# Two block products of the first expert product, each by seven products of their own blocks

## The chip, the cores and the metric

The kernel runs on one core of a Trainium2 chip. Its time is device microseconds (us) of one execution, the median over runs. The engines are TensorE (PE for matmuls, PEld for its weight loads), VectorE (DVE), ScalarE (ACT), GpSimd (POOL) and SyncE (SP, which issues most DMAs). Each engine works through its own queue; semaphores order the queues among each other. Matmuls write PSUM[...].

## The reference

A modulated projection of `x` gives the token rows `y` (4096 rows of 512). A router scores each row for 8 experts; every expert takes the 1024 rows that it scores highest, and adds its gated two-layer network to them:

```python
scores = jax.nn.softmax(xt @ Wr, axis=-1)
G, idx = jax.lax.top_k(scores.T, k)
X_in = xt[idx]
h = jax.nn.gelu(jnp.einsum('ekd,edh->ekh', X_in, W1) + b1[:, None, :], approximate=False)
X_e = jnp.einsum('ekh,ehd->ekd', h, W2) + b2[:, None, :]
contrib = (G[..., None] * X_e).reshape(E * k, D)
out = jnp.zeros((N, D), dtype=x.dtype).at[idx.reshape(-1)].add(contrib)
```

All of it is float32. Here k = 1024, D = 512 and the hidden width is 2048.

## The kernel before

The first 180 us or so make `y`, the scores and the rows of expert 0. After that the kernel is a row of 16 equal passes: 8 experts, and for each expert two halves `p` of the hidden width. A pass is a **hidden stage** (`X_in @ W1` for 1024 hidden columns, bias and Gelu into the buffer `H`) and an **output stage** (`H @ W2`, scaled by the gate and added to the output rows by an indirect DMA).

Both products are done as 2 x 2 blocks by seven block products in place of eight (Winograd's form). For the hidden stage the token matrix is split into two halves of 512 tokens and two of 256 inputs, the weights into two halves of inputs and two of 512 hidden columns. DVE makes four sums of token blocks once an expert (`left_sums`, called from `prepare`, line 948) and four sums of weight blocks per pass (`weight_sums`, line 195). The last one is made in place, in block `0,1`.

A hidden stage is four units (`hidden_unit`, line 342 on), each 128 of the 512 columns of a half. A unit is seven products, in the order p1, p2, p6, p7, p5, p3, p4. Each product is two matmuls of 128 x 512 (inputs 0 to 127 and 128 to 255). p1, p6, p5 and p3 add up in one bank `a`; ACT copies the bank out between them (`snap`, line 1059). p2 has bank `b`, p7 and p4 share a bank `c`. DVE adds the copies to `b` and `c`, and ACT's Gelu writes the four quarters of `H`. An output unit (`out_unit`, line 1102, four per pass) has the same form: seven products of four matmuls of 128 x 256, with sums of `H` blocks in four tiles of its own.

The helper `in_turns` (line 1012) sets the order on PE: p1 of a unit, then p3 of the unit before, p2, p4 of the unit before, p6, p7, p5. At the end of a stage the last p3 and p4 are issued. Between units it calls other work: the sums of the weights that come next, `fetch` (indices and gathers of the next expert's rows, in the hidden stage of `p` = 1) and `prepare` (in the output stage of `p` = 1). Every matmul of both stages stands in `product` (line 1028), so the profile gives them all that line, and the tiles tell them apart: `ps_a_h`, `ps_b_h`, `ps_c_h` in a hidden stage, `ps_a_o`, `ps_b_o`, `ps_c_o` in an output stage. A scheduling layer can move an instruction past others of its engine; the order in the profile is what it left.

`fetch` first makes the indices: DVE builds a one-hot tile `oh` of 32 x 128 columns (line 849), and PE multiplies it in 32 small bfloat16 matmuls. Then eight indirect DMAs gather rows into `row` tiles (four buffers), SP writes them to a DRAM tile and reads them back in a layout for DVE's transposes. The main loop loads `W1` of the next pass after the hidden stage and `W2` of the next pass after the output stage (lines 1222 and 1228).

Of the kernel before, what the change touches and what calls it, by code (L numbers as in the profile page):

```python
# [20 lines left out]
P = 128  # L21
# [4 lines left out]
def tile_modulated_expert_choice_ffn(  # L26
# [75 lines left out]
    NL = P // E  # L102
    pk = const.tile([P, P], I32, name="pk")
    nc.gpsimd.iota(pk, pattern=[[0, P]], base=0, channel_multiplier=1)
    pm = const.tile([P, P], I32, name="pm")
    nc.gpsimd.iota(pm, pattern=[[1, P]], base=0, channel_multiplier=0)
    ek = const.tile([P, P], I32, name="ek")
    nc.vector.tensor_scalar(ek, pk, E - 1, None, op0=ALU.bitwise_and)
    em = const.tile([P, P], I32, name="em")
    nc.vector.tensor_scalar(em, pm, E - 1, None, op0=ALU.bitwise_and)  # L110
    same = const.tile([P, P], BF16, name="same")
    nc.vector.tensor_tensor(same, ek, em, ALU.is_equal)
    ahead = const.tile([P, P], BF16, name="ahead")
    nc.vector.tensor_tensor(ahead, pk, pm, ALU.is_lt)
    nc.vector.tensor_mul(ahead, ahead, same)

# [47 lines left out]
    U = HP // 2  # L164
    QD = D // 2
    w1_blocks, w2_blocks = {}, {}

# [27 lines left out]
    def weight_sums(kind, blk, name):  # L195
        for _ in weight_sum_steps(kind, blk, name):
            pass

    def load_w1(e, ps):
# [537 lines left out]
    def route_others():  # L737

        ST = rt.tile([P, 2, P], F32, tag="ST", name="ST")
        ps = ps_t.tile([P, 2, P], F32, tag="t", name="ps_ST")  # L740
# [13 lines left out]

        mark = rt.tile([P, 2, P], F32, tag="run", name="mark")
        cand = two_bits[:, 0, :]
# [17 lines left out]
        def ranks(mask, name):  # L774

            run = rt.tile([P, 2, P], F32, tag="run", name=f"run_{name}")
            nc.vector.tensor_tensor_scan(run.rearrange("p h t -> p (h t)"),
# [14 lines left out]

        sel = rt.tile([P, 2, P], F32, name="sel")
        cnt = rt2.tile([P, 1], BF16, tag="cnt", name="cnt_gt")
        nc.vector.tensor_scalar(sel, ST, thr, None, op0=ALU.is_gt, op1=ALU.add, accum_out=cnt)
        tot = total(cnt, "gt")
        eq = rt.tile([P, 2, P], F32, name="eq")
        nc.vector.tensor_scalar(eq, ST, thr, None, op0=ALU.is_equal)
# [18 lines left out]
        for h in range(2):  # L817
            nc.tensor.transpose(ps[:, h, :], pos[:, h, :], ident)

        pos_i = rt.tile([P, NT, E], I32, tag="ST", name="pos_i")  # L820
        nc.vector.tensor_scalar(pos_i.rearrange("p t e -> p (t e)"),
                                ps.rearrange("p h m -> p (h m)"), -1.0, None, op0=ALU.add)
        part = rt.tile([P, NT, E], I32, tag="part", name="part")
        nc.vector.tensor_scalar(part, pos_i, P - 1, None, op0=ALU.bitwise_and)
        lo = rt.tile([P, NT, E], BF16, name="lo")
        nc.vector.tensor_copy(lo, part)
        part2 = rt.tile([P, NT, E], I32, tag="part", name="part2")
        nc.vector.tensor_scalar(part2, pos_i, 7, None, op0=ALU.logical_shift_right)
        hi = rt.tile([P, NT, E], BF16, name="hi")
        nc.vector.tensor_copy(hi, part2)  # L830
        for e in range(1, E):
            places[e] = lo[:, :, e], hi[:, :, e]

    def indices(e):
# [13 lines left out]
        )  # L848
        nc.vector.tensor_tensor(  # L849
            oh, lo.unsqueeze(2).to_broadcast([P, NT, P]),  # L850
            iota_lo.unsqueeze(1).to_broadcast([P, NT, P]), ALU.is_equal,
        )
        ps = ps_small.tile([P, 2, KG], F32, tag="small", name=f"ps_idx{e}")
# [50 lines left out]
    def gather(e, i):  # L904
# [5 lines left out]
        for j in range(GH):  # L910
            g = i * GH + j
            to = gp.tile([P, YW], F32, tag="row", name=f"row_{e}_{g}", bufs=4)
            sent = nc.gpsimd.indirect_dma_start(
                out=to[:, :], out_offset=None, in_=y_dram[:, :],
                in_offset=bass.IndirectOffsetOnAxis(ap=idx[:, e, g : g + 1], axis=0),
            )
            nc.sync.dma_start(rows[j * P : (j + 1) * P, :], to)
# [18 lines left out]
    def token_tiles(e):  # L936
# [7 lines left out]
        return xT, s, gain, ngain  # L944

    def prepare(e):

        xT, s, gain, ngain = token_tiles(e)
        for i in range(2):
            xg = gathered.pop((e, i))  # L950
            for k in range(2):
                nc.vector.transpose(
                    xT[i, k].rearrange("p j (t b) -> p t j b", b=TB),
                    xg[:, :, 2 * k * TB : 2 * (k + 1) * TB].rearrange("p t (j a) -> p t j a", a=TB))
        nc.vector.tensor_scalar_mul(ngain, gain, -1.0)
        left_sums(xT[0, 0], xT[0, 1], xT[1, 0], xT[1, 1], s)

    def first_tokens(started):
# [39 lines left out]

    def in_turns(units, between):

# [4 lines left out]
        for n in range(len(units)):  # L1005
# [12 lines left out]
            for work in between.get(n, ()):  # L1018
                with tc.issue_after(mark.ins):
                    work()  # L1020
            held = unit[5:]
        for f in held:
            f()

    def product(ps, lefts, rights, start):
        n = len(lefts)
        for k in range(n):
            nc.tensor.matmul(ps, lefts[k], rights[k], start=(start and k == 0), stop=(k == n - 1),  # L1028
                             skip_group_check=True)

    def hidden_unit(e, p, u, H, early=False):
# [8 lines left out]
        def mm(ps, left, right, start):  # L1040
            s = tokens[e][0]
            product(ps, [blk[right][:, k, u * P : (u + 1) * P] for k in range(2)],
                    [s[left][:, k, :] for k in range(2)], start)

        def begin(cols):
            s = tokens[e][0]
# [10 lines left out]
        def snap(n):  # L1057
            t = sp.tile([P, HALF], F32, tag=f"snap{n}", name=f"snap{n}_{name}")
            nc.scalar.copy(t, st["a"])  # L1059
# [7 lines left out]

        def p2():
            if not early:
                st["b"] = bank("b", name, 1)  # L1070
                mm(st["b"], "12", (1, 0), True)
            added = nc.vector.tensor_add(st["b"], st["b"], st["s1"])  # L1072
            nc.scalar.activation(out[0, 0], st["b"], AF.Gelu, bias=bias[0])
            return added
# [5 lines left out]
        def p7():  # L1080
            st["c"] = bank("c", name, 2)
            mm(st["c"], "s3", "t3", True)

        def p5():
# [9 lines left out]
        def p4():  # L1094
            mm(st["c"], "22", "t4", False)
            nc.vector.tensor_add(st["c"], st["c"], st["u2"])
            nc.scalar.activation(out[1, 0], st["c"], AF.Gelu, bias=bias[0])

        unit = [p1, p2, p6, p7, p5, p3, p4]
        return (begin, unit) if early else unit  # L1100

    def out_unit(e, p, v, H, b2_sb):
# [5 lines left out]
        a = {(i, k): H[:, :, k, i * HALF + c : i * HALF + c + P] for i in range(2) for k in range(2)}  # L1108
        s = {n: sp.tile([P, U, P], F32, tag=f"h{n}", name=f"h{n}_{name}")
             for n in ("s1", "s2", "s3", "s4")}  # L1110
        left_sums(a[0, 0], a[0, 1], a[1, 0], a[1, 1], s)
# [93 lines left out]
    for e in range(E):  # L1205
        b2_sb = fx.tile([P, D], F32, tag="b2", name=f"b2_{e}")
        nc.sync.dma_start(b2_sb, b2[e, :].partition_broadcast(P))
        for p in range(NP):
# [6 lines left out]
            if p == NP - 1 and e + 1 < E:  # L1215
                work[0] = [partial(fetch, e + 1)]
            units = [partial(hidden_unit, e, p, u, H) for u in range(U)]
            if e == p == 0:
                units[0:2] = [lambda unit=unit: unit for _, unit in early]
            in_turns(units, work)  # L1220
            if nxt[0] < E:
                load_w1(*nxt)
            work = {GH - 2: [partial(sums, "w1", w1_blocks, nxt)]}
            if p == NP - 1 and e + 1 < E:
                work[0] = [partial(prepare, e + 1)]
            in_turns([partial(out_unit, e, p, v, H, b2_sb) for v in range(GH)], work)
            if nxt[0] < E:
                load_w2(*nxt)

# [39 lines left out]
```

## Time and profile before

The time is 1750.95 us, the median of three runs (1750.62 to 1751.68).

| | |
|---|---|
| the profiled execution's own time | 1745.7 us |
| its span, first to last instruction | 1743.9 us |
| mean granted TensorE clock | 0.996 |
| distance of the first hidden products of two passes, `p` = 0 | 96.90 us |
| the same, `p` = 1 (with the index matmuls) | 98.01 us |

A group row of the profile has the line, engine, operation, tiles and shapes, then busy time and the mean length of one operation in ns, and the engine's idle time just before them with what ended it. A timeline row has the start in us, the length, and how many instructions are merged into it. The page's chain of waits goes back from the last instruction to what released each step.

### The profile page before, as it was taken

Reading aid. Unit: us, or ns where it says so; the run is one execution under the profiler, and the core shown is the slowest. Engines: PE = TensorE matmul, PEld = TensorE weight load, DVE = VectorE, ACT = ScalarE, POOL = GpSimd, SP = SyncE. Lnnn points to the kernel's source line nnn. Section 1 sums busy time; section 2 is a strip of 40 time slices with the busy share of each in tenths; the row PEclk is TensorE's granted clock in tenths of the full one; section 3 lists DMA queues with packets and bytes.
Section 4 is the critical chain, followed back from the end, with each engine's and each line's share of the span. In section 5 each row is a group of like instructions: output and inputs, shape, how many; then the busy total and the mean of one; then the engine's idle time right before and its main releaser. Section 6 shows DMA issues by size and latency. Waiting matters only on the chain.

```text
span 1743.9 us, 17415 instructions
## 1 busy us (share of the span) xinstructions
PE 1718.0 (99%) x6646; PEld 1136.2 (65%) x6646; DVE 830.8 (48%) x1467; ACT 480.2 (28%) x845; POOL 293.5 (17%) x238
## 2 busy tenths in 40 slices
PE   9998999999999999999999999999999999999997
PEld 5775475665748485766758485766758484756656
DVE  5885884524535254624535254614444254614341
ACT  3543312223131322222231313222231313222231
POOL 0112013020212013110312012110302012110202
PEclk9999999999999999999999999999999999999999
DMA  9625527441574237442574237432564137332403
GB/s 207 171 50 197 192 55 179 106 85 49 97 201 73 48 61 183 90 85 55 100 191 85 49 63 176 90 79 55 112 179 90 46 64 186 75 79 61 85 0 49
DMA packets 143252, 178.59 MB, mean 102 GB/s; under 512 B 16825, under 2 KB 92857, under 8 KB 143041
## 3 DMA queue, kind: packets, MB, share of 16 engines
q1 hardware_dynamic: 118240, 115.19, 24.4%
q0 software_dynamic: 24912, 62.27, 21.0%
q8 instruction: 52, 0.85, 0.2%
q14 instruction: 32, 0.25, 0.0%
q10 hardware_dynamic: 16, 0.02, 0.0%
HBM read 120.46 MB, written 65.37 MB: 107 GB/s over the span
## 4 chain that ended last, share of the span: by engine, by line
PE 93%; DVE 4%; ACT 1%; issue 1%; DMA 1%; POOL 0%; POOLq 0%; DVEq 0%; ACTq 0%
PE ps_a_o L1028 25%; PE ps_a_h L1028 23%; PE ps_c_o L1028 12%; PE ps_c_h L1028 12%; PE ps_b_o L1028 6%; PE ps_b_h L1028 6%; PE ps_ya L81 2%; PE ps_yc L81 1%; DVE oh L849 1%; PE ps_y L81 1%; ACT xmT L500 1%; DVE mark L760 1%; PE ps_yt L727 1%; PE ps_a_h_a L1028 0%; PE ps_yb L81 0%
## 5 line engine op out<-in xcount | busy, mean ns | idle before, releaser
L1156 POOL DMA_INDIRECT out<-o_o,idx x128 | 213.2, 1666 | 1246.7 <-DVE o_o L1153 497.0
L1028 PE MATMUL ps_a_o<-w_t,hs_o 128*128 128x256 f32 x1024 | 243.3, 380 | 1.2
L1028 PE MATMUL ps_a_h<-xs,w_t 128*128 128x512 f32 x496 | 233.4, 592 | 0.0
L1028 PEld LDWEIGHTS ps_a_o<-w_t,hs_o 128*128 128x128 f32 x1024 | 192.3, 190 | 33.7 <-issue 7.2
L1028 PEld LDWEIGHTS ps_a_h<-xs,w_t 128*128 128x128 f32 x496 | 94.1, 190 | 119.1 <-issue 118.5
L1059 ACT COPY snap_h<-ps_a_h 128x512 f32<-128x512 f32 x186 | 108.2, 582 | 230.0 <-PE ps_a_h L1028 227.0
L1123 ACT ACTIVATE snap_o<-ps_a_o,gain 128x256 f32<-128x256 f32 x128 | 60.6, 474 | 346.7 <-PE ps_a_o L1028 346.7
L1087 DVE TENSOR_TENSOR snap_h<-snap_h,ps_c_h 128x512 f32<-128x512 f32 x64 | 43.9, 687 | 217.5 <-ACT snap_h L1059 217.5
L1072 DVE TENSOR_TENSOR ps_b_h<-ps_b_h,snap_h 128x512 f32<-128x512 f32 x62 | 43.4, 699 | 202.6 <-PE ps_b_h L1028 202.6
L1028 PE MATMUL ps_c_o<-w,hs_o 128*128 128x256 f32 x512 | 124.2, 380 | 0.0
L1028 PE MATMUL ps_a_o<-w,H 128*128 128x256 f32 x512 | 124.0, 379 | 0.0
L1028 PE MATMUL ps_a_o<-w,hs_o 128*128 128x256 f32 x512 | 121.6, 380 | 0.0
L1028 PE MATMUL ps_b_o<-w,H 128*128 128x256 f32 x512 | 121.1, 379 | 0.0
L1028 PE MATMUL ps_a_h<-xT,w 128*128 128x512 f32 x248 | 120.7, 594 | 0.0
L1028 PE MATMUL ps_c_h<-xs,w 128*128 128x512 f32 x256 | 120.5, 593 | 0.0
L1028 PE MATMUL ps_c_h<-xT,w_t 128*128 128x512 f32 x256 | 120.5, 593 | 0.0
L1028 PE MATMUL ps_c_o<-w_t,H 128*128 128x256 f32 x504 | 119.1, 379 | 0.0
L1028 PE MATMUL ps_a_h<-xs,w 128*128 128x512 f32 x248 | 118.2, 599 | 0.0
L1028 PE MATMUL ps_b_h<-xT,w 128*128 128x512 f32 x248 | 116.8, 593 | 0.0
L1028 PEld LDWEIGHTS ps_a_o<-w,H 128*128 128x128 f32 x512 | 97.1, 190 | 27.0 <-issue 15.5
L1028 PEld LDWEIGHTS ps_a_o<-w,hs_o 128*128 128x128 f32 x512 | 95.9, 190 | 21.8 <-ACT snap_o L1123 9.2
L1028 PEld LDWEIGHTS ps_c_o<-w,hs_o 128*128 128x128 f32 x512 | 97.0, 190 | 13.9 <-issue 0.6
(277 smaller groups left out, 1983.8 us busy)
## 6 DMA issues: line engine op xcount, KB each, us to landing
w<-in_w SPq DMA_DIRECT2D x120, 512.0 KB, 4.1
rows<-row SPq DMA_DIRECT2D x56, 260.0 KB, 3.9
xg<-rows SPq DMA_DIRECT2D x56, 256.0 KB, 6.4
x<-in_x SPq DMA_DIRECT2D x28, 256.0 KB, 8.4
y_dram<-ytok SPq DMA_DIRECT2D x5, 1024.0 KB, 4.3
w<-in_w SPq DMA_DIRECT2D x32, 128.0 KB, 3.5
y_dram<-ytok POOLq DMA_DIRECT2D x12, 256.0 KB, 5.0
b<-in_b SPq DMA_DIRECT2D x8, 256.0 KB, 4.2
```

Source lines behind the costliest of these rows:

```text
L81: behind[engine] = make()
L500: nc.scalar.mul(t, t, styles[1][:, j, b : b + 1])
L727: nc.tensor.transpose(ps[:, o * P : (o + 1) * P], yT[:, o, t * P : (t + 1) * P], ident)
L760: nc.vector.tensor_scalar(mark, ST, cand[:, c + 1 : c + 2].bitcast(F32), None, op0=ALU.is_ge, op1=ALU.add, accum_out=cnt[:, c : c + 1])
L849: nc.vector.tensor_tensor(oh, lo.unsqueeze(2).to_broadcast([P, NT, P]), iota_lo.unsqueeze(1).to_broadcast([P, NT, P]), ALU.is_equal,)
L1028: nc.tensor.matmul(ps, lefts[k], rights[k], start=(start and k == 0), stop=(k == n - 1), skip_group_check=True)
L1059: nc.scalar.copy(t, st["a"])
L1072: added = nc.vector.tensor_add(st["b"], st["b"], st["s1"])
L1087: nc.vector.tensor_add(st["u4"], st["u4"], st["c"])
L1123: nc.scalar.mul(t, st["a"], scale)
L1156: nc.gpsimd.indirect_dma_start(out=last_rows[g] if e == E - 1 else out_rows, out_offset=bass.IndirectOffsetOnAxis(ap=idx[:, e, g : g + 1], ...
```

## The change

In 15 of the 16 hidden stages (all but the first) the products p2 and p4 of the four units are no longer made unit by unit. Together, p2 of all units is one product of a token block (512 tokens x 256 inputs) with a weight block (256 inputs x 512 columns), and so is p4. Each is now split once more into 2 x 2 blocks and made by seven products: 128 inputs, 256 tokens, and 2 x 128 hidden columns. A group (`second_level`) makes the seven products for 128 columns of each half, each in a single matmul of 128 x 256, and leaves the result in an SBUF tile `q`; four groups (`which` 2 and 4, `r` 0 and 1) serve a stage. Units take their quarter from `q`, in place of a bank.

`hidden_stage` is the new order: the other five products of the units 0, 2, 1, 3 fill 21 slots, and after each of the first 16 slots one step of a group follows (two products, or one). The last p3 and p4 of an output stage are kept back (`keep`) and issued in the slots of the next hidden stage; the loads of `W2` follow them there.

The sums of the second level are made on DVE: `second_sums` for the tokens, eight of 256 columns once an expert, and eight per pass in `weight_sums`. To make room, several tiles share buffers: the tokens' sums take the buffer of `xT10`, three sums of an output unit take the buffers of the hidden units' copies and the fourth is written over a block of `H`, the routing tiles of the first pass take the `row` buffers (three in place of four), and the tiles of the start are freed after use. The one-hot of `indices` is made in four pieces.

```diff
@@ weight_sums
+        if kind == "w1":
+            bases = {2: blk[1, 0], 4: blk["t4"]}
+            t = wpool.tile([P, 3 * len(bases), Q], F32, tag="w1_l2", name=f"w1_l2_{name}")
+            for m, (which, base) in enumerate(bases.items()):
+                b = {(k, j): base[:, k, j * Q : (j + 1) * Q] for k in range(2) for j in range(2)}
+                t1, t2, t4 = [t[:, 3 * m + n, :] for n in range(3)]
+                nc.vector.tensor_add(t1, b[0, 0], b[0, 1])
+                nc.vector.tensor_add(t2, t1, b[1, 1])
+                nc.vector.tensor_add(t4, t2, b[1, 0])
+                nc.vector.tensor_add(b[0, 1], b[0, 1], b[1, 1])
+                blk["l2", which] = {**b, "t1": t1, "t2": t2, "t3": b[0, 1], "t4": t4}
@@ indices
-        nc.vector.tensor_tensor(
-            oh, lo.unsqueeze(2).to_broadcast([P, NT, P]),
-            iota_lo.unsqueeze(1).to_broadcast([P, NT, P]), ALU.is_equal,
-        )
+        for n in range(4):
+            here = slice(n * NT // 4, (n + 1) * NT // 4)
+            nc.vector.tensor_tensor(
+                oh[:, here, :], lo[:, here].unsqueeze(2).to_broadcast([P, NT // 4, P]),
+                iota_lo.unsqueeze(1).to_broadcast([P, NT // 4, P]), ALU.is_equal,
+            )
@@ gather
-            to = gp.tile([P, YW], F32, tag="row", name=f"row_{e}_{g}", bufs=4)
+            to = gp.tile([P, YW], F32, tag="row", name=f"row_{e}_{g}", bufs=3)
@@ new functions
+    def second_sums(e):
+        s = tokens[e][0]
+        t = fx.tile([P, 4, Q], F32, tag="xT10", name=f"x2_{e}")
+        more = fx.tile([P, 2, Q], F32, tag="x2", name=f"x2_more_{e}")
+        free = [t[:, n, :] for n in range(4)] + [more[:, n, :] for n in range(2)]
+        for m, which in enumerate((2, 4)):
+            base = s["12" if which == 2 else "22"]
+            a = {(i, k): base[:, k, i * Q : (i + 1) * Q] for i in range(2) for k in range(2)}
+            s2 = {n: free[3 * m + j] for j, n in enumerate(("s2", "s3", "s4"))}
+            s2["s1"] = a[1, 0]
+            left_sums(a[0, 0], a[0, 1], a[1, 0], a[1, 1], s2)
+            s["l2", which] = {**s2, "11": a[0, 0], "12": a[0, 1], "22": a[1, 1]}
+
+    def second_level(e, p, which, r):
+        ...
+        def mm(tag, left, right, start):
+            if start:
+                st[tag] = (bank("b", f"q{name}", 1) if tag == "b" else
+                           ps_t.tile([P, HALF], F32, tag="t", name=f"ps_q{tag}_{name}"))[:, 0:Q]
+            product(st[tag], [blk[right][:, r * P : (r + 1) * P]], [s[left]], start)
+        ...
+        def p5():
+            mm("a", "s1", "t1", False)
+            st["u4"] = snap(4, -1.0)
+            nc.vector.tensor_sub(out[1, 1], st["u4"], st["c"])
+        ...
+        return [p1, p2, p6, p7, p5, p3, p4], q
+
+    def hidden_stage(e, p, H, between, held, then):
+        unit = {u: hidden_unit(e, p, u, H) for u in range(U)}
+        slots = []
+        for n, u in enumerate((0, 2, 1, 3)):
+            p1, _, p6, p7, p5, p3, _ = unit[u]
+            slots += [p1, held[0], p6] + ([held[1]] if n == 0 else []) + [p7, p5]
+            held = [p3]
+        ends = {5: 0, 10: 1, 15: 2, 20: 3}
+        steps, q = [], {}
+        for r in range(2):
+            for which in (2, 4):
+                g, q[which, r] = second_level(e, p, which, r)
+                steps += [g[0:2], g[2:4], g[4:5], g[5:7]]
+        finish = {3: (2, 0), 6: (2, 2), 7: (4, 0), 9: (4, 2), 12: (2, 1), 15: (4, 1), 16: (2, 3),
+                  19: (4, 3)}
+        mark = None
+        for n, f in enumerate(slots):
+            f()
+            if n == 3:
+                then()
+            for step in steps[n] if n < len(steps) else ():
+                mark = step() or mark
+            if n in finish:
+                which, u = finish[n]
+                unit[u][1 if which == 2 else 6](q[which, u % 2][:, u // 2, :])
+            for work in between.get(ends.get(n), ()):
+                with tc.issue_after(mark.ins):
+                    work()
+        for f in held:
+            f()
@@ hidden_unit
-        def p2():
-            if not early:
-                st["b"] = bank("b", name, 1)
-                mm(st["b"], "12", (1, 0), True)
-            added = nc.vector.tensor_add(st["b"], st["b"], st["s1"])
-            nc.scalar.activation(out[0, 0], st["b"], AF.Gelu, bias=bias[0])
+        def p2(other=None):
+            to = st["s1"] if other is not None else st["b"]
+            added = nc.vector.tensor_add(to, st["b"] if other is None else other, st["s1"])
+            nc.scalar.activation(out[0, 0], to, AF.Gelu, bias=bias[0])
             return added
...
         def p7():
             st["c"] = bank("c", name, 2)
             mm(st["c"], "s3", "t3", True)
+            if e or p:
+                nc.vector.tensor_add(st["u2"], st["u2"], st["c"])
...
+        def finish_p4(other):
+            nc.vector.tensor_add(st["u2"], st["u2"], other)
+            nc.scalar.activation(out[1, 0], st["u2"], AF.Gelu, bias=bias[0])
@@ out_unit
-        s = {n: sp.tile([P, U, P], F32, tag=f"h{n}", name=f"h{n}_{name}")
-             for n in ("s1", "s2", "s3", "s4")}
+        s = {n: sp.tile([P, HALF], F32, tag=f"snap{t}", name=f"h{n}_{name}").rearrange(
+            "p (k m) -> p k m", m=P) for n, t in (("s2", 1), ("s3", 2), ("s4", 4))}
+        s["s1"] = a[1, 0]
@@ main loop
-            units = [partial(hidden_unit, e, p, u, H) for u in range(U)]
             if e == p == 0:
+                units = [partial(hidden_unit, e, p, u, H) for u in range(U)]
                 units[0:2] = [lambda unit=unit: unit for _, unit in early]
-            in_turns(units, work)
+                in_turns(units, work)
+            else:
+                hidden_stage(e, p, H, work, held, partial(load_w2, e, p))
             if nxt[0] < E:
                 load_w1(*nxt)
...
-            in_turns([partial(out_unit, e, p, v, H, b2_sb) for v in range(GH)], work)
-            if nxt[0] < E:
-                load_w2(*nxt)
+            if e == p == 0:
+                work[0] = [partial(second_sums, 0)]
+            held = in_turns([partial(out_unit, e, p, v, H, b2_sb) for v in range(GH)], work,
+                            keep=nxt[0] < E)
```

## The prediction

> **What bounds the kernel now.** I read the page first: the span, the busy shares and the chain that ended last.
>
> ```profile
> span 1743.9 us, 17415 instructions
> PE 1718.0 (99%) x6646; PEld 1136.2 (65%) x6646; DVE 830.8 (48%) x1467; ACT 480.2 (28%) x845; POOL 293.5 (17%) x238
> PEclk9999999999999999999999999999999999999999
> PE 93%; DVE 4%; ACT 1%; issue 1%; DMA 1%; POOL 0%; POOLq 0%; DVEq 0%; ACTq 0%
> ```
>
> PE (TensorE) is busy 99% of the span at full granted clock, and 93% of the chain is its own work. Only fewer or shorter matmuls, or fewer PE waits, can move the time. Next, the groups by line, for the price of one operation of each width.
>
> ```profile
> L1028 PE MATMUL ps_b_h<-xT,w 128*128 128x512 f32 x248 | 116.8, 593 | 0.0
> L1028 PE MATMUL ps_b_o<-w,H 128*128 128x256 f32 x512 | 121.1, 379 | 0.0
> L1123 ACT ACTIVATE snap_o<-ps_a_o,gain 128x256 f32<-128x256 f32 x128 | 60.6, 474 | 346.7 <-PE ps_a_o L1028 346.7
> L1072 DVE TENSOR_TENSOR ps_b_h<-ps_b_h,snap_h 128x512 f32<-128x512 f32 x62 | 43.4, 699 | 202.6 <-PE ps_b_h L1028 202.6
> ```
>
> Every f32 matmul is two records (62 products of two matmuls give x248). The means 593 and 379 ns are latencies, which overlap; the price is the distance between starts, so I went to PE's timeline, at the seam between a hidden stage and its output stage.
>
> ```profile
> 510.58 1.88 PE L1028 MATMUL ps_c_h<-xs,w 128*128 128x512 f32 x4
> 512.30 1.88 PE L1028 MATMUL ps_a_h<-xs,w_t 128*128 128x512 f32 x4
> 514.02 1.03 PE L1028 MATMUL ps_a_o<-w,H 128*128 128x256 f32 x4
> 514.91 1.98 PE L1028 MATMUL ps_a_h<-xs,w 128*128 128x512 f32 x4
> 516.73 1.88 PE L1028 MATMUL ps_c_h<-xT,w_t 128*128 128x512 f32 x4
> 518.45 1.03 PE L1028 MATMUL ps_a_o<-w,H 128*128 128x256 f32 x4
> 519.31 1.89 PE L1028 MATMUL ps_b_o<-w,H 128*128 128x256 f32 x8
> 521.04 1.03 PE L1028 MATMUL ps_c_o<-w,hs_o 128*128 128x256 f32 x4
> 522.15 1.97 PE L1028 MATMUL ps_a_o<-w_t,hs_o 128*128 128x256 f32 x8
> ```
>
> From 510.58 to 514.02 are two 512-wide products: 1.717 us each, **0.858 us a matmul**. A 256-wide product (x8, four matmuls) takes 1.727 us elsewhere in the same timeline (529.99 to 531.72), **0.432 us a matmul**. The ratio is 0.503.
> The reader is also to see what is lost here: 521.04 to 522.15 is 1.11 us for work of 0.86, a wait of 0.25 us for DVE's second sum of the first output unit, and 0.10 us at 514.91 to 516.73.
>
> **The sum, part by part.**
>
> *Products.* In 15 of 16 hidden stages the products 2 and 4 of four units go: 2 x 4 x 1.717 = 13.74 us. In come 4 groups x 7 = 28 matmuls of 256 columns: 28 x 0.432 = 12.09 us. A stage saves 1.65 us, all on the chain; 15 stages **-24.7 us**. Ends for the new matmul: the trace has none that is a product by itself between 512-wide ones. From below, no row is cheaper than 0.432. From above, a weight load that isn't hidden: PEld's row is 190 ns, and 0.622 us each would add 80 us. I take 0.432: where the old stages change width (562.80, two records of 512, to 563.66; 567.14 to 568.00) the 512-wide start distance stays 0.86 us.
> A rule speaks against this. The Trainium skill, "TensorE: Matmul & The Clock Gate", section "Back-to-back issue gap", gives a stream of weight load and matmul pairs as about 81 ns at 128 columns and 131 ns at 512: narrowing saves little. A straight line puts 256 at 98 ns, a ratio of 0.75; the new matmul would then be 0.64 us (an estimate from that page), a stage 28 x 0.64 = 17.9 us against 13.7, the whole +63 us. The row says 0.503 for f32, where the 190 ns load fits under each record's 216 ns. The row decides.
>
> *The seam.* Product 4 with its late add and Gelu no longer ends the stage; the order of after has product 5 and product 3 of unit 3 last, and product 2 of the output unit ahead of product 6. From the end of product 5: ACT copy 0.8, DVE add to 1.5, Gelu to 2.3, then two DVE sums of 0.69 to 3.8; PE has 1.3 + 1.72 + 0.43 + 1.73 = 5.2 us of other work there. The 0.25 us wait and the 0.07 us after it go; the 0.13 us around the interleaved product 3 stay. 15 seams x 0.27 = **-4 us** (ends: 0 and -5).
>
> *The index matmuls.* The one-hot of 4.42 us on DVE (seven times) becomes four pieces, and the 32 small matmuls of PE become four lots between 512-wide matmuls. The nearest row for one lot is `tot_b` in the first stage: 0.03 us itself, and the next product takes 1.80 instead of 1.72, so 0.11; three more lots are 0.33. The first lot waits for the value tiles: from the end of the second group's product 2, DVE does an add (to 0.65), hot 0.42, one piece 1.1, and 0.28 + 0.42, about 3.0 us; PE has 2.6 us of work. That is a wait of 0.4 where the trace has 0.2. 7 x 0.5 = **+3.5 us** (ends: -1, if the pieces hide better, and +7).
>
> *ACT and DVE in the hidden stage.* New on ACT are 16 copies of 0.474 us = 7.6 on top of some 18.1 (12 copies, 16 Gelus): 26 of 46 us. On DVE 12 adds of about 0.48 and four of 0.69: 13.2 becomes 21.7 us. Neither is a bound in sum; what counts is who waits in the queue. Second-level accumulations come at least 2.1 us after the copy they overwrite, four times its length. The tight place is after the w2 sums (4.9 us on DVE, unmoved in slot). Behind them stand unit 1's two adds and the add of its product 4; ACT's Gelu waits for the last, and behind that Gelu stands the copy of unit 3's product 1, which product 6 must have. From the end of the fourth group's product 2: DVE is through at 9.2, the Gelu at 9.95, the copy at 10.55; PE wants it at 10.75. One more 0.1 us is in the later copy before product 3. I charge 0.15 us a stage, **+2 us** (ends: 0, and 0.5 a stage, 7).
>
> *Output stage.* On DVE eight 256-wide sums for the weights (each stage) and eight for the tokens (each expert) are new: 0.42 each, 3.4 + 3.4 us, beside 48 us of PE work of which DVE fills 25 to 29 now. They stand ahead of the add that frees bank `b`: for the third output unit I count that add done at 22.7 us, wanted at 25.9. Cost nothing; without that cover some 0.5 us, 7 times. The sum s1 written into H and the h sums in the snap buffers remove no wait and add none: their last readers are at least a unit back.
>
> *Moves.* SP: the w2 loads now stand behind the last output product, in front of the row copies as before, and land (4.1 us) some 25 us before their sums. With three row buffers instead of four the gathers run in three rounds; the first transposed rows stand behind a w1 load that waits for the middle of the stage. Cover: the second half's rows were and are queued behind the load of `w1_01`, free one and a half products before the end of the stage; issued 2 us and landed 6.4 us later they are 5 us early for DVE's transposes. If not, DVE holds the output sums and PE waits. The routing tiles in shared buffers and the scoped start tiles keep DVE's order; first loads wait for nothing: 0. The first hidden stage is unchanged on PE.
>
> Sum: -24.7 - 4 + 3.5 + 2 = **-23 us**. The profiled run was 1745.7 us (span 1743.9), so it would become 1722.5. The median of the runs shown is 1750.95, 5.3 above the profiled one; the same saving puts it at **1727.7 us**.
>
> **The rivals.**
> 1. *Slower: the narrow matmul shows its weight load.* Each of the 28 is one matmul with a semaphore wait; were the load held until the wait is met, 0.19 us x 28 x 15 = 80 us come in: 1808. The gain is gone from 23 us / 420 = 55 ns a matmul. For it: 514.91, where a just-met wait cost 0.1 us. Against: each output product begins with such a wait, and its eight records still keep 216 ns.
> 2. *The queues hold PE.* ACT's order has ten more places where a Gelu stands before a copy; 0.8 us more a stage is 12 us: 1740. For it: slack of 0.2 us at one place. Against: the other places have 0.5 us or more.
> 3. *The rows come late.* Three buffers and the loads in front cost more than 5 us; 2 us in 7 stages is 14 us: 1742. Against: DVE's transposes show no idle time before them now.
> 4. *It saves nothing*, since some 1.8 us a stage comes back in sum from 1 to 3: about 1751.
>
> **Chances.** The forecast 0.72, with its own range of 1720 to 1736 (the ends above). Rival 1: 0.07; rival 2: 0.11; rival 3: 0.05; rival 4: 0.05. The range for 8 in 10 is 1718 to 1740: the forecast and the near half of rival 2. About 0.2% (3.5 us) is what a measurement of this kernel can tell from no change. Faster 0.87, within 0.2% 0.04, slower 0.09.
>
> **What would show it.** In the profile after: 256-wide groups for the new tiles with 0.43 us between starts; a period of about 95 us without indices and 97 with them, where it is 96.9 and 98.0 now; a seam without the 0.25 us gap; four lots of index matmuls. Wrong would be: PEld idle behind the q tiles at each step (rival 1), PE waiting for the copies of h (rival 2), or DVE idle before the transposes (rival 3).

## The result, and the profile after

After took 1722.65 us (median of four runs, 1721.19 to 1724.97) where before took 1751.32 (four runs, 1750.62 to 1752.43): ratio 0.9837, 95% interval 0.982 to 0.9854, 28.7 us less. The forecast was 1727.7 us.

The page of after, with the span, the busy time and the clock by slices, and the chain of waits by engine and by line:

```profile
span 1721.7 us, 18925 instructions
PE 1692.2 (98%) x7006; PEld 1211.3 (70%) x7006; DVE 1004.0 (58%) x1912; ACT 553.1 (32%) x1085; POOL 310.4 (18%) x238
PEclk9999999999999999999999999999999999999999
PE 93%; DVE 3%; ACT 1%; DMA 1%; issue 1%; another core or an unknown queue 0%; POOLq 0%; POOL 0%; SPq 0%; DVEq 0%; ACTq 0%
```

PE lost 26 us of busy time although it has 360 more matmul records; DVE took on 173 us and ACT 73 us, and neither has a larger share of the chain than before. PE is still the bound.

The places named beforehand, in PE's timeline of after. First the second level among the 512-wide products (start, length, instructions merged):

```profile
576.81 1.88 PE L1063 MATMUL ps_a_h<-xs,w_t 128*128 128x512 f32 x4
578.52 0.59 PE L1063 MATMUL ps_qa<-x,w_l 128*128 128x256 f32 x2
578.95 0.59 PE L1063 MATMUL ps_qc<-x_more,w_t 128*128 128x256 f32 x2
579.39 1.02 PE L1063 MATMUL ps_a_h<-xT,w 128*128 128x512 f32 x2
```

The starts 578.52, 578.95 and 579.39 show that the new matmul costs 0.43 us, and the 512-wide product before it keeps its 1.71. Then the seam to the output stage:

```profile
612.47 1.46 PE L1063 MATMUL ps_a_o<-w,H 128*128 128x256 f32 x6
613.77 1.94 PE L1063 MATMUL ps_a_h<-xs,w 128*128 128x512 f32 x4
615.54 0.59 PE L1063 MATMUL ps_a_o<-w,H 128*128 128x256 f32 x2
615.98 1.89 PE L1063 MATMUL ps_b_o<-w,H 128*128 128x256 f32 x8
617.70 1.89 PE L1063 MATMUL ps_a_o<-w_t,hs_o 128*128 128x256 f32 x8
619.43 1.89 PE L1063 MATMUL ps_c_o<-w,hs_o 128*128 128x256 f32 x8
```

The third product (617.70) follows the second by 1.72; the gap of 0.25 us is gone, and of the 0.13 around product 3 only 0.05 is left (613.77 to 615.54 is 1.77).

The length of a pass is read as the distance of the first hidden products of two passes. The first rows of three passes before, one without indices and then one with them:

```profile
562.80 1.02 PE L1028 MATMUL ps_a_h<-xT,w 128*128 128x512 f32 x2
659.70 1.02 PE L1028 MATMUL ps_a_h<-xT,w 128*128 128x512 f32 x2
757.71 1.02 PE L1028 MATMUL ps_a_h<-xT,w 128*128 128x512 f32 x2
```

The same passes after:

```profile
564.32 1.88 PE L1063 MATMUL ps_a_h<-xT,w 128*128 128x512 f32 x4
659.14 1.88 PE L1063 MATMUL ps_a_h<-xT,w 128*128 128x512 f32 x4
755.30 1.88 PE L1063 MATMUL ps_a_h<-xT,w 128*128 128x512 f32 x4
```

A pass became 94.82 us without indices (96.90 before, so 2.08 less) and 96.15 with them (98.01; over the seven, 1.85 less). From the first whole hidden product to the end the profiles differ by 7 x 1.85 (passes with indices) + 2.36 + 6 x 2.08 (without; the first of these was 97.18 before) + 2.08 (the last, to the end of the span) - 0.14 (the first) = **29.7 us**. The two profiled executions differ by only 22 us: that of after reached its first whole hidden product at 200.13 us, that of before at 192.68, with the same PE program up to there. So the experiments had two questions: what makes up the 29.7, and whether the 7.45 us belong to the change.

### The profile page after: what moved, and what is told of

Read it like the earlier page. It is cut to its first block, busy times and chain, and to the rows that moved or that the text cites. A ratio compares the mean times of both kernels' runs of the same rounds, so it can differ in the third digit from the quotient of the medians.

```text
span 1721.7 us, 18925 instructions
## 1 busy us (share of the span) xinstructions
PE 1692.2 (98%) x7006; PEld 1211.3 (70%) x7006; DVE 1004.0 (58%) x1912; ACT 553.1 (32%) x1085; POOL 310.4 (18%) x238
## 4 chain that ended last, share of the span: by engine, by line
PE 93%; DVE 3%; ACT 1%; DMA 1%; issue 1%; another core or an unknown queue 0%; POOLq 0%; POOL 0%; SPq 0%; DVEq 0%; ACTq 0%
PE ps_a_o L1063 25%; PE ps_a_h L1063 25%; PE ps_c_o L1063 13%; PE ps_c_h L1063 6%; PE ps_b_o L1063 6%; PE ps_qa L1063 6%; PE ps_qc L1063 3%; PE ps_ya L81 2%; PE ps_b_q L1063 2%; PE ps_yc L81 1%; PE ps_y L81 1%; ACT xmT L514 1%; DVE spare L777 1%; PE ps_yt L741 1%; PE ps_a_h_a L1063 0%
## 5 line engine op out<-in xcount | busy, mean ns | idle before, releaser
L1294 POOL DMA_INDIRECT out<-o_o,idx x128 | 223.7, 1748 | 1140.2 <-DVE o_o L1291 488.4
L1063 PE MATMUL ps_a_o<-w_t,hs_o 128*128 128x256 f32 x512 | 121.2, 379 | 0.0
L1063 PE MATMUL ps_a_o<-w_t,H 128*128 128x256 f32 x512 | 121.2, 379 | 0.0
L1063 PE MATMUL ps_a_h<-xT,w 128*128 128x512 f32 x248 | 117.1, 594 | 0.0
L1063 PEld LDWEIGHTS ps_a_o<-w_t,H 128*128 128x128 f32 x512 | 97.1, 190 | 13.7 <-issue 0.5
L1063 PEld LDWEIGHTS ps_a_o<-w_t,hs_o 128*128 128x128 f32 x512 | 97.2, 190 | 13.2
L1063 PEld LDWEIGHTS ps_b_o<-w,H 128*128 128x128 f32 x512 | 97.2, 190 | 13.2
L1063 PEld LDWEIGHTS ps_c_o<-w_t,H 128*128 128x128 f32 x504 | 95.8, 190 | 13.0
```

Of the source, the lines that this page charges most:

```text
L1294: nc.gpsimd.indirect_dma_start(out=last_rows[g] if e == E - 1 else out_rows, out_offset=bass.IndirectOffsetOnAxis(ap=idx[:, e, g : g + 1], ...
```

## The experiments

Twelve runs in three turns; the kernels of a turn ran on one chip, beside runs of before.

| turn | kernel | median us | ratio to before, 95% |
|---|---|---|---|
| 1 | before (16 runs) | 1746.17 | |
| 1 | before again | 1746.7 | 1.0 (0.9991 to 1.0009) |
| 1 | seam alone | 1739.9 | 0.9968 (0.9955 to 0.998) |
| 1 | copy later | 1716.87 | 0.9831 (0.9818 to 0.9845) |
| 1 | one piece | 1714.54 | 0.9814 (0.9801 to 0.9828) |
| 2 | before (13 runs) | 1750.33 | |
| 2 | after again | 1721.31 | 0.9833 (0.982 to 0.9847) |
| 2 | 128 columns | 1727.07 | 0.9864 (0.9849 to 0.9879) |
| 2 | whole products | 1744.76 | 0.9967 (0.9958 to 0.9977) |
| 2 | later and one piece | 1720.54 | 0.9828 (0.9815 to 0.9841) |
| 3 | before (15 runs) | 1745.28 | |
| 3 | before beside | 1746.07 | 1.0002 (0.9993 to 1.0012) |
| 3 | after beside | 1716.39 | 0.9834 (0.9819 to 0.9849) |
| 3 | one piece again | 1713.13 | 0.9817 (0.9803 to 0.983) |
| 3 | copies twice | 1717.29 | 0.9837 (0.9822 to 0.9852) |

Before itself takes 1745 to 1746 us in two turns and 1750 in the other; so times are compared within a turn, and small differences by the distances of passes, which repeat to 0.05 us from the fourth on, except that in after a pass with indices is now and then 0.1 us longer.

### The seam alone

In before, the last unit of a hidden stage takes the order of after's end; all products stay.

```diff
+        def last_p7():
+            p7()
+            nc.vector.tensor_add(st["u2"], st["u2"], st["c"])
+        def last_p4():
+            b = bank("b", name + "_p4", 1)
+            mm(b, "22", "t4", True)
+            nc.vector.tensor_add(b, b, st["u2"])
+            nc.scalar.activation(out[1, 0], b, AF.Gelu, bias=bias[0])
         unit = [p1, p2, p6, p7, p5, p3, p4]
+        if u == U - 1:
+            unit = [p1, p2, p6, last_p7, p5, last_p4, p3]
```

> Before, with one part of the change done alone: in the last unit of a hidden stage product 4 goes ahead of product 3, into bank b, and its late add no longer ends the stage. Products stay as in before. Theory (the seam is worth what the trace of after lets me read, some 0.3 to 0.45 us a pass): 16 x 0.3 to 0.45 = 5 to 7 us less, about 1745 us, ratio 0.996 to 0.997; no gap of 0.25 us behind the third product of the first output unit. Rival (the 0.43 us a pass that after saves beyond its products comes from elsewhere, such as the output stage or the turns of the second level): 0 to 1 us less, ratio 0.9995 to 1.000.

It took 6.3 us less. Passes are 96.45 and 97.56 us, 0.45 less each; the first pass, which takes the new order too, is 0.87 us longer (77.80 for 76.93). PE's timeline of this kernel at the seam:

```profile
513.75 1.88 PE L1028 MATMUL ps_b_h_p<-xT,w_t 128*128 128x512 f32 x4
515.47 1.88 PE L1028 MATMUL ps_a_h<-xs,w 128*128 128x512 f32 x4
517.18 1.89 PE L1028 MATMUL ps_a_o<-w,H 128*128 128x256 f32 x8
518.91 1.89 PE L1028 MATMUL ps_b_o<-w,H 128*128 128x256 f32 x8
520.64 1.89 PE L1028 MATMUL ps_a_o<-w_t,hs_o 128*128 128x256 f32 x8
```

Every product starts 1.71 to 1.73 us after the one before: no gap, and product 3 is no longer cut into the output product. All of the seam, 0.25 + 0.07 + 0.13 = 0.45 us, was there to be had without the second level.

What the 0.13 was is told by PEld's waits for ACT's copies of bank `a`, in ten passes of before (the run "before beside"; total us, times, longest):

```profile
PEld ps_a_h L1028 <- ACT snap_h L1059: 2.7, 10, 0.3
```

That is one wait a pass, and it stands at the seam: product 3 adds to the bank that ACT copies out behind product 5, and before has only 0.86 us of other matmuls between the two (514.02 to 514.91 in the prediction's rows). Here a whole product stands between them, and the trace has no such row.

### The products undone, the order kept

In after, each group makes products 2 and 4 of its two units whole, in its own slots.

```diff
-        def mm(tag, left, right, start):
...
-        return [p1, p2, p6, p7, p5, p3, p4], q
+        def whole(j):
+            def f():
+                ps = (bank("b", f"q{name}", 1) if j == 0 else
+                      ps_t.tile([P, HALF], F32, tag="t", name=f"ps_qa_{name}"))
+                c = (2 * j + r) * P
+                product(ps, [blk[:, k, c : c + P] for k in range(2)],
+                        [s[:, k, :] for k in range(2)], True)
+                return nc.vector.tensor_copy(q[:, j, :], ps)
+            return f
+        return [whole(0), nothing, whole(1), nothing, nothing, nothing, nothing], q
```

> After, with the products undone and the order kept: at the slots of the second level stand products 2 and 4 of two units, two 512-wide matmuls each as in before, copied by DVE into the same tiles; the second-level copies and adds are gone (the sums are still made). Theory (the saving outside the seam is that of the products alone, 13.74 - 12.09 = 1.65 us a stage): 15 x 1.65 = 24.7 us above after, and 4 to 7 us below before, ratio to before 0.996 to 0.9975. Rival (the finer turns of after, one bank more in flight, save something of their own): less than 20 us above after, ratio under 0.9945. Second rival (the queues cost the second level something that is gone here): more than 26 us is not gained back, that is, under 22 us above after with passes at 96.0 us or less.

The lines shown leave out that the fourth weight sum is written over the first one and no longer over a quarter of the block. The token sums of the second level are still made, and one of them is written over a quarter of each token block that these products then read; so the values are not those of the reference, but the work is the same in size and only the time is used. The time is 23.5 us above after. Passes without indices are 96.47 us, **1.65 above after's 94.82**, the number of the prediction, and 0.43 below before, the seam. Passes with indices are 97.62, 1.47 above after's: here the index matmuls fall differently. Over the stages this is 8 x 1.65 + 7 x 1.47 = 23.5. Neither rival holds: the turns of the second level save nothing beyond their products, and their queues cost nothing that came back.

### The price of a narrow matmul

```diff
-            product(st[tag], [blk[right][:, r * P : (r + 1) * P]], [s[left]], start)
+            for c in (0, P):
+                nc.tensor.matmul(st[tag][:, c : c + P], blk[right][:, r * P : (r + 1) * P],
+                                 s[left][:, c : c + P], start=(start and c == 0), stop=True,
+                                 skip_group_check=True)
```

> After, with each of the 28 second-level matmuls of a stage cut into two of 128 columns, same work and same weights. Theory (time goes by columns down to this width: in the trace of before the early products of the first tokens, 128 wide, stand 0.447 us apart for two matmuls, 0.223 each): 2 x 0.223 in place of 0.432, 0.014 more, x 28 x 15 = 6 us above after, ratio to before about 0.9865. Rival 1 of the prediction (a new weight load that is not hidden, 0.19 us a record, four records in place of two): 4 x 0.19 = 0.76 in place of 0.432, 0.33 more, x 420 = 138 us above after, ratio near 1.06. The ratio of the skill's issue gaps (81 ns for 128 columns against some 98 for 256, estimate) would make it 0.432 x 2 x 81 / 98 = 0.71, 118 us above after.

5.8 us above after; expected were 6. In PE's timeline of this kernel each row with x4 is one matmul of after in two halves:

```profile
574.82 0.61 PE L1080 MATMUL ps_qa<-xT,w_t 128*128 128x128 f32 x4
575.26 0.61 PE L1080 MATMUL ps_b_q<-xT,w_t 128*128 128x128 f32 x4
575.71 1.88 PE L1063 MATMUL ps_a_h<-xs,w_t 128*128 128x512 f32 x4
```

0.445 us for the pair of halves, 0.222 each, against 0.432 for the whole. For these f32 matmuls the time goes by columns down to 128, with 0.013 us for the cut. Rival 1 is out: with 420 more matmuls, 840 more weight loads stay hidden. The ratio of the sustained figures in the Trainium skill, "TensorE: Matmul & The Clock Gate", section "Back-to-back issue gap", would have given some 118 us (an estimate from that page, with a straight line to 256 columns); the 5.8 us measured here do not agree with it.

### The one-hot in one piece, twice

```diff
-        for n in range(4):
-            here = slice(n * NT // 4, (n + 1) * NT // 4)
-            nc.vector.tensor_tensor(
-                oh[:, here, :], lo[:, here].unsqueeze(2).to_broadcast([P, NT // 4, P]),
-                iota_lo.unsqueeze(1).to_broadcast([P, NT // 4, P]), ALU.is_equal,
-            )
+        nc.vector.tensor_tensor(
+            oh, lo.unsqueeze(2).to_broadcast([P, NT, P]),
+            iota_lo.unsqueeze(1).to_broadcast([P, NT, P]), ALU.is_equal,
+        )
```

> After, with one part undone: the one-hot of an expert's indices is made in one piece instead of four. Theory (four lots of index matmuls cost 0.23 us an expert more than one lot, as the distances of the passes say): 7 x 0.23 = 1.6 us less, about 1721 us; a pass with indices is near 95.9 us instead of 96.15. Rival (as the prediction had it, four lots cost 0.5 us an expert more): 3.5 us less, about 1719 us, a pass of 95.65 us. Second rival (the pieces hide the one-hot, and one piece makes TensorE wait): 5 us more or worse, above 1727 us, a pass of 96.9 us or longer.

> After with the one-hot in one piece, once more, beside after on one chip, since the first run of it had none beside it. Theory: passes with indices 95.83 us against 96.15 us, 7 x 0.32 = 2.2 us below after; ratio to before 0.9818 to 0.982, the best of the versions. Rival (the one piece pays elsewhere): no more than 1 us below after.

Passes with indices go from 96.15 to 95.83 us in both runs, 7 x 0.32 = 2.2 us; the medians of turn 3 differ by 3.3 us, whose intervals as ratios overlap. So four lots cost more than one, not less. The single lot of before, in PE's timeline:

```profile
671.77 1.02 PE L1028 MATMUL ps_a_h<-xT,w 128*128 128x512 f32 x2
672.83 0.97 PE L855 MATMUL ps_idx<-val,oh 128*128 128x16 bf16 x32
673.65 1.10 PE L1028 MATMUL ps_a_h<-xT,w 128*128 128x512 f32 x2
674.60 1.88 PE L1028 MATMUL ps_a_h<-xs,w 128*128 128x512 f32 x4
```

Two of the four lots of after:

```profile
673.78 0.59 PE L1063 MATMUL ps_qc<-x_more,w_t 128*128 128x256 f32 x2
674.38 0.36 PE L871 MATMUL ps_idx<-val,oh 128*128 128x16 bf16 x8
674.60 1.96 PE L1063 MATMUL ps_a_h<-xT,w 128*128 128x512 f32 x4
676.40 0.35 PE L871 MATMUL ps_idx<-val,oh 128*128 128x16 bf16 x8
676.60 0.68 PE L1063 MATMUL ps_qa<-xT,w_l 128*128 128x256 f32 x2
```

The single lot of "one piece again", behind a 512-wide product that starts at 667.79:

```profile
669.61 0.96 PE L869 MATMUL ps_idx<-val,oh 128*128 128x16 bf16 x32
670.43 0.68 PE L1061 MATMUL ps_qa<-x_more,w_t 128*128 128x256 f32 x2
```

The small matmuls themselves cost the same: a lot of eight takes 0.20 to 0.22 us from its start to the next product (674.38 to 674.60, 676.40 to 676.60), and the single lot of 32 takes 0.82. What each lot adds is 0.08 us in the product behind it (674.60 to 676.40 is 1.80, not 1.72; 673.65 to 674.60 is 0.95, not 0.86). Three more lots are 0.24. The rest is the wait for the first lot: 0.20 us in before (671.77 + 0.86 to 672.83), 0.17 in after (673.78 + 0.43 to 674.38), 0.10 here (667.79 + 1.72 to 669.61). So a pass with indices is 1.10 us longer than one without in before, by these rows; 1.31 in after; 1.00 here. The distances of the passes say 1.11, 1.33 and 1.01. The one-hot of 4.4 us is hidden because the single lot stands behind three more products than the first lot of after. This is the best of the versions, 1713.1 us in turn 3.

### Room in ACT's queue

```diff
                 mm(st["a"], "11", (0, 0), True)
+            if e or p:
+                nc.scalar.copy(H[:, u, 0, 0:HALF], st["a"])
             st["s1"] = snap(1)
```

> After, with one more ACT copy of 0.59 us ahead of the copy behind product 1 of each hidden unit (60 in all; it writes a quarter of H that Gelu writes over later). It measures the room in ACT's queue. The prediction counted 0.2 us of room at the copy of unit 3 and charged 0.15 us a stage. If that count is right: 0.4 us a stage or more come back, 15 x 0.4 = 6 us above after, ratio to before 0.9865. If there is more room (the passes of after leave 0.04 us for all waits): the passes stay within 0.1 us of 94.82 and 96.15 us, under 1.5 us above after.

Passes are 94.96 and 96.30 us, 0.14 longer (15 x 0.14 = 2.1 us), and the median is 0.9 us above after. That lies between the two expectations, by far nearer to the second. PEld's waits for ACT in ten passes (total us, times, longest), of after and then of this kernel:

```profile
PEld ps_a_h L1063 <- ACT snap_h L1185: 4.3, 20, 0.2
```

```profile
PEld ps_a_h L1063 <- ACT snap_h L1185: 11.6, 30, 0.7
```

A third wait a pass has come in. The added 0.59 us costs 0.14 in all four places of a stage together, so the tightest place had at least 0.45 us of room, where the prediction counted 0.2.

### Before and after again: do the 7.45 us belong to the change?

In the first profile of after DVE and ACT stood still at 171 to 175 us, while PE waited. Three pairs of runs asked why.

> The kernel before, unchanged, profiled once more. The profile of after shows, at 171 to 175 us, DVE and ACT standing still before the copies of the third group of first tokens, and a granted clock near 0.50 for the 6 us behind it; there the first hidden stage begins 7.45 us later (200.13 us instead of 192.68). Theory (that hole belongs to the execution, not to the change): among the executions of before it is there too, so the profile taken now has the hole, a first hidden stage near 200 us and a time near 1751 us, or it hasn't, and then its time is near 1745.7 us; the ratio is 1.000. Rival (the change makes the hole): the first hidden stage begins near 192.7 us again although the time is near 1751 us.

Before, unchanged, has no such stand-still in this profile; its index matmuls for the first tokens start 4.4 us later than in the first profile of before (162.15 us instead of 157.76), its first whole hidden product comes at 198.14 us, and its passes are 96.90 and 98.01 as ever. Its ten runs go from 1745.02 to 1751.17 us. So the part ahead of the passes varies by 6 us without any change, but this run didn't show the stand-still itself.

> After, unchanged, beside before on one chip. The profiles give a saving from the first whole hidden product to the end of 7 x 1.85 (passes with indices) + 2.36 + 6 x 2.08 (without) + 2.03 (the last) - 0.14 (the first) = 29.7 us. Theory (that is all of it; what comes before the first hidden stage varies from run to run and is the same for both kernels in the median): ratio 0.983, about 29 to 30 us below before whatever before takes on this chip. Rival (the change makes the part before the first hidden stage longer, by up to the 7.45 us of its first profile): 22 to 25 us below, ratio 0.986 to 0.987.

The time is 29.0 us less, a ratio of 0.9833, as the theory had it. The stand-still is there.

> Before, profiled on the same chip and in the same turn as after. On the chip of the first turn (before 1746.2 us) no profile showed a stand-still of DVE and ACT near 171 us; on that of the second (before 1750.3 us) all four kernels that hold the change showed it, and none of before was taken there. Theory (the stand-still goes with the chip or the load of the program): before and after show it both, or neither; before is near 1750 us with it and near 1746 us without it. Rival (it goes with the change): only after shows it. Ratio 1.000.

> After, profiled beside that. Theory: it shows the stand-still if before does; from the first whole hidden product to the end 29.7 us less than before whichever it is; ratio 0.983. Rival: it shows it alone, and the ratio is then 0.985 to 0.987.

Here neither shows it. The first whole hidden product comes at 192.27 us in before and 192.59 in after; the spans are 1743.2 and 1714.3, 28.9 apart, as the medians are. From the first whole hidden product to the end the difference is 29.2 us, not the 29.7 of the first pair: the passes repeat, but the stretch behind the last first hidden product goes from 107.1 to 107.7 us in three profiles of after. So the change by itself doesn't make the stand-still. Whether before has it on the chip of turn 2 was not profiled; but the saving is 28.7, 29.0 and 28.9 us in the three places, whether after stood still or not, so the 7.45 us are not a cost of the change.

The 8 MB copy of the input into the output, which is issued at about that time, was my suspect. The edit that issues it later:

```diff
-        with tc.issue_after(sent.ins):
-            nc.gpsimd.dma_start(
-                out.rearrange("b l d -> b (l d)").rearrange("b (r w) -> (b r) w", r=16),
-                x.rearrange("b l d -> b (l d)").rearrange("b (r w) -> (b r) w", r=16))
...
-                nc.scalar.copy(gain[:, i * GH : (i + 1) * GH], half[i][:, :, D])
+                sent = nc.scalar.copy(gain[:, i * GH : (i + 1) * GH], half[i][:, :, D])
+        with tc.issue_after(sent.ins):
+            nc.scalar.dma_start(
+                out.rearrange("b l d -> b (l d)").rearrange("b (r w) -> (b r) w", r=16),
+                x.rearrange("b l d -> b (l d)").rearrange("b (r w) -> (b r) w", r=16))
```

> After, with the 8 MB copy of the input into the output issued from ACT's queue behind the last copies of the first tokens, in place of POOL's queue behind the gathers. Theory (the stand-still of DVE and ACT at 171 to 175 us, and the low clock after it, come from that copy's traffic): both are gone, the first hidden stage begins near 193 us, the time is some 5 to 7 us under after, about 1716 to 1718 us, ratio to before 0.980 to 0.981. Rival (the hole has another cause, such as the start or the fetching of instructions): the hole stays at its place, the time stays within 2 us of after, 1722 us, ratio 0.983 to 0.984. Second rival: the hole moves behind the copy's new place and the time stays.

> After with both edits: the one-hot in one piece (passes with indices at 95.83 us, 7 x 0.32 = 2.2 us less) and the 8 MB copy from ACT's queue behind the first tokens' copies. Theory (the copy beside the gathers delays the first tokens): about 2.2 us from the first and 2 to 4 us from the second below after, ratio to before 0.980 to 0.981, and the best of all. Rival (the copy costs the same wherever it stands, and the run without a hole was luck): 2.2 us below after, ratio 0.982.

In turn 1 the kernel with the later copy had no stand-still, but neither had any other of that turn; the 76.09 us of its first pass, 1.0 less, are more than given back ahead of it (15.9 us from the start of the last early product to that of the first whole one, 14.6 in "after beside"). In turn 2, with the copy out of the way, the stand-still stays in place, and the time is 0.8 us below after, within the spread, although this kernel also has the one-hot in one piece. DVE and PE of that run:

```profile
170.71 0.42 DVE L946 SCALAR_TENSOR_TENSOR xs<-xs,xT 128x256 f32<-128x256 f32 x1
174.81 0.76 DVE L1012 COPY xT<-ps_xg 128x256 f32<-128x256 f32 x2 [3.68 <-remote]
```

```profile
170.66 1.19 PE L81 MATMUL ps_xg<-ident,xg 128*128 128x128 f32 x8
175.29 1.10 PE L81 MATMUL ps_a_h_a<-xT,w 128*128 128x128 f32 x4 [3.44 <-DVE xT L1012]
```

The copy is not its cause. The order of time in the first trace of after speaks against it too: DVE stands still from 171.20 us on, but the copy is issued at 173.41 and its first packet moves at 175.15. The fetch of instructions, a rival named beforehand, isn't told apart either: its 16 KB transfer near that time (173.31 us in after, 171.22 in "after beside") is there in every profile, with the stand-still and without. All five profiles with it hold the change, and four of them are of turn 2, where before was not profiled (its time there, 1750.3, is 4 to 5 us above the other turns', as after's is). What holds DVE and ACT is open.

## Why the prediction was right, point by point

| term | predicted | measured | from |
|---|---|---|---|
| products | -24.7 | -24.7 | 1.65 a stage (without indices), "whole products" against after |
| seam | -4 | -6.5 | 0.43 a pass x 15; 0.45 in "seam alone" |
| index matmuls | +3.5 | +1.6 | 7 x (2.08 - 1.85) |
| ACT and DVE queues | +2 | about 0 | 20 x 1.717 + 28 x 0.432 + 28 x 1.727 = 94.79; measured 94.82 |
| sum | -23 | -29.6 | the traces: -29.7 and -29.2; the medians: -28.7 to -29.0 |

The bound and the place of each saving were right. The three terms besides the products were all set too dear, by 6.6 us together, so the forecast lies 5 us above the measured time, inside its range.

**Products: right to the hundredth.** The price from start distances (0.858 and 0.432) was the one that held. The ratio of the issue gaps, as the prediction cites it, would have turned the sign; the row decided against it, and "128 columns" shows the row's kind of price down to half the width.

**Seam: right in kind, mis-sized.** "The 0.13 us around the interleaved product 3 stay" is the step that failed. That loss was a wait for ACT's copy behind product 5, and the order of after puts 1.30 us of other matmuls (612.47 to 613.77) where before had 0.86; 0.05 is left. In "seam alone" it is a whole product, and all 0.45 us go.

**Index matmuls: mis-sized.** Both parts were too dear. The 0.11 a lot counted the small matmul of `tot_b` itself, which the 32 index matmuls cost in any number of lots; without it a lot adds 0.08, three lots 0.24 for 0.33. And the wait for the first lot did not grow by 0.2: it is 0.17 (before 0.20). Against before's one lot it came to 0.23 where 0.5 was charged.

**Queues: charged for nothing.** The count at unit 3's copy left 0.2 us of room and I charged 0.15 for it; the room is 0.45 us or more, by "copies twice".

**Output stage, moves.** They cost nothing, as said. DVE's transposes of the gathered rows still begin without idle time (last column), so three `row` buffers and the loads in front of them are early enough:

```profile
L983 DVE STREAM_TRANSPOSE xT<-xg 128x1024 f32<-128x1024 f32 x28 | 33.1, 1218 | 0.0
```

**Reference point and range.** The profiled execution of before was 5.3 us under the median of its runs, and I carried that over as an offset. That stands: the medians of before differ by 5 us between turns, and the saving does not. The range was summed wrongly: the ends of the terms give 1720 to 1740, not 1736; the result lies inside either.

**Rivals.** 1 (visible weight load): refuted by the 0.43 between starts and by "128 columns". 2 (queues hold PE): even 60 more copies cost only 0.14 us a stage. 3 (rows late): the row above. 4 (nothing saved): refuted by the time.

## What to carry to other kernels

Price a narrower matmul by the distance between starts of that width and type in the kernel's own trace, not by a figure that names no type. At a seam, ask for every small loss which wait it is, and how much other work the new order puts in front of it: here 6.3 us of a saving of some 29 needed only another order of products. Cutting a hidden producer into pieces also cuts its consumer into lots, and each lot adds a loss of its own (0.08 us here): one piece, placed later, was 0.3 us cheaper each time.

## What was not expected of the hardware

Behind the stand-still PE ran at half clock. In the first profile of after, this row ends the wait of PE:

```profile
175.10 1.22 PE L81 MATMUL ps_a_h_a<-xT,w 128*128 128x128 f32 x4 [3.29 <-DVE xT L1018]
```

The windows of that profile, and then of "after beside", show the clock (us, PE, PEld, DVE, ACT, POOL busy with counts, granted clock, DMA share, GB/s):

```profile
171.00:175.00 4.00, 0.81 (x8) 0.57 (x6) 0.58 (x3) 0.32 (x2) 2.50 (x3) 0.93 0.77 204
176.00:178.00 2.00, 2.00 (x11) 2.00 (x11) 0.81 (x3) 0.00 (x0) 0.00 (x0) 0.50 0.41 172
179.00:180.00 1.00, 1.00 (x7) 1.00 (x6) 0.22 (x1) 0.00 (x0) 0.00 (x0) 0.50 0.54 197
```

```profile
171.00:175.00 4.00, 3.92 (x36) 3.68 (x35) 3.33 (x10) 0.65 (x2) 1.49 (x2) 1.00 1.14 405
176.00:178.00 2.00, 1.92 (x18) 1.80 (x17) 1.92 (x7) 1.53 (x6) 0.00 (x0) 1.00 1.25 492
```

PE idles 3.29 us, and then the clock is 0.50 until past 180 us; early products that start 0.45 us apart in "after beside" start 0.86 apart here. From the start of the first early product to that of the last it is 10.69 us in "after beside" (167.29 to 177.98) and 16.52 here (168.99 to 185.51), so a wait of 3.3 us costs some 5.8. The Trainium skill, "TensorE: Matmul & The Clock Gate", Part 1, gives an idle window of about 3.4 us as the trigger. That fits: the idle times of the five profiles with the stand-still are 3.29 to 3.52 us, and in "after beside" PE idles 0.76 us at most near there and keeps its clock.
